# Two convolution banks emptied by ScalarE alone: offsets in the base's upper channels, the odd half through SBUF

## The chip, the cores and the metric

One core of a Trainium2 chip (trn2) runs the whole program. The metric is the device time of one execution in microseconds. Five engines work side by side, each in the order of its own program: PE (TensorE, matrix products; its weight loads are shown apart as PEld), DVE (VectorE), ACT (ScalarE), POOL (GpSimd) and SP (SyncE, which here only issues DMAs). They wait for each other through semaphores.

## What is computed

Two layers over 32 images of 96 x 56 x 56. The first is an inverted bottleneck (1x1 to 576 channels, 3x3 depthwise, squeeze and excite, 1x1 back to 96). The second attends in channels and space by the magnitudes of a Fourier transform, and then mixes a plain and a deformable 3x3 convolution. The change touches only this part of the second layer:

```
aux = concatenate([y, coord, freq_e], 1)                  # 96 + 5 channels
offset = conv3x3(aux, off_w, off_b)                       # 18 channels
gate = sigmoid(conv1x1(relu(conv3x3(aux, dg1_w, dg1_b)), dg2_w, dg2_b))   # 50 hidden
y_base = conv3x3(y, base_w, base_b)                       # 96 channels
y_def = deformable 3x3 convolution of y at the offsets    # 96 channels
z = (1 - gate) * y_base + gate * y_def
out = relu(batchnorm(z) + x)
```

All data is float32.

## The kernel before

**Images and bands.** An image is cut into 7 bands of 8 rows (448 pixels), so there are 224 bands. A band passes three stages: the *joint and base convolutions* that make its hidden gate values, its offsets and its base (two bands ahead of their use); the *sampling*, in two halves, in which small matrix products with bilinear weights (L718) make the values at the offset positions; and the *deformable product* (L737) with the combination (L776 to L779). Beside the bands of image b run the attention of image b+1 (L387, L408 and what follows; its projection is L325, L331, L335, L463) and the depthwise convolution of image b+2: L166 on PE expands, L170 on ACT applies SiLU, L257 and L259 on DVE add the nine taps (long instructions over 128 x 1568), and L219 on ACT finishes a unit after its last tap.

**Order.** The program is written as generators that are stepped side by side: `offsets` for a band is stepped once for every tile of the sampling, and after each step `pump` advances the other streams by their share. The order on PE, DVE, ACT and POOL is then set by the framework's list scheduler from dependencies and priorities; on SP it is the order of the text. On each engine it is fixed when the program is built: an instruction that waits holds up all behind it.

**PSUM.** All products but three kinds go to the pool `mm` of six banks (`bank`), which are handed out in turn. A matmul into a bank waits until the last reader of its former contents is done.

**The joint convolution** (`joint_conv`, L617 to L635). Nine taps (L602, `conv3`) over 104 channels (96 of y, 5 auxiliary ones, 3 planes that add each pixel's place and the offsets' bias) fill one bank of 128 rows: rows 0 to 49 the hidden values, rows 64 to 81 the 18 offsets (`OFF0` is 64), rows 96 to 127 the base's last 32 channels (`QC` is 32; `BC` is 64). ACT takes the hidden values out (L622) and, in a later step, the 32 base channels with their bias (L625, into `yb`). DVE takes out the offsets in two strided copies of 18 x 224 (L648, into `at`). ACT's L625 comes after DVE's copies, since both read one bank.

**The base convolution** of the first 64 channels (L630) lets even taps add up in rows 0 to 63 of a second bank and odd taps in rows 64 to 127. ACT takes out the even half with the bias (L633, into `yb[:64]`); in the next step DVE adds the odd half straight from the bank (L635). So the last reader of the first bank is ACT's L625 and that of the second bank is DVE's L635.

**The way of the offsets.** After L648 POOL issues a DMA of the offsets to DRAM (L652, `od`); SP loads them back broadcast (L664, `ht`), ACT turns them into weights per axis (L667, L668), ACT's queue stores these (L671, `hd`), SP loads them as column and row weights (L682, L683: `wc`, `wr`), and DVE multiplies the two (L689). That product is an input of the sampling L718. L659 on DVE keeps the largest offset (`top`), which decides at the end of all bands whether a general path must run.

**Others that the prediction names.** L700 (POOL) and L704 (PE) cut y into blocks and transpose them; L706 (ACT) empties those two banks. L722 (ACT) empties the banks of L718, L729 (ACT) packs part of the values, and both feed L737. L394 (ACT) is a PSUM copy of the transform, L482 and L483 (DVE) are two small SBUF copies of the attention, L274 (`sa`) and L518 (`cx`) late DVE steps of the attention, after which L528 on PE goes on.

Of the kernel before, what the change touches and what calls it, by code (L numbers as in the profile page):

```python
# [7 lines left out]
FP = mybir.dt.float32  # L8
I32 = mybir.dt.int32
AF = mybir.ActivationFunctionType  # L10
ALU = mybir.AluOpType
# [5 lines left out]
C, H, W = 96, 56, 56  # L17
# [9 lines left out]
CA = C + 5  # L27
CJ = CA + 3
NOFF, NTAP = 18, 9
# [5 lines left out]
NBD = H // RB  # L35
BW = NBW
TS = 4
NTX = W // TS
NTH = NTX // 2
TP = TS * TS  # L40
GROUPS = ((0, 3),), ((3, 5), (5, 7))
REACH = PD
SB = TS + 2 * REACH
NS = SB * SB
KP = NTAP * TP
BC = 64
QC = 32
KA = 7
DMID = CA // 2
OFF0 = 64  # L50
MAUX = OFF0 + NOFF
MID = C // 4
PT = 2 * W
# [61 lines left out]
def bank(p):  # L115
    return p["mm"].tile([128, 512], FP, name="mm")
# [479 lines left out]
def conv3(nc, out, weights, yp, channels, j):  # L596

    view = out.rearrange("p (h w) -> p h w", h=RB)
    for k in range(NTAP):
        dy, dx = divmod(k, 3)  # L600
        r0 = j * RB + dy + PD - 1
        nc.tensor.matmul(view, weights[:, k], yp[:channels, r0 : r0 + RB, dx + PD - 1 : dx + PD - 1 + W],  # L602
                         start=(k == 0), stop=(k == NTAP - 1))


def aux_conv(nc, p, yp, j):

    w = p["w"]
    pa = bank(p)
    conv3(nc, pa[:MAUX, :BW], w["aux"], yp, CA, j)  # L610
    hid = p["hid"].tile([DMID, BW], FP, name="hid")
    nc.scalar.activation(hid, pa[:DMID, :BW], AF.Relu, bias=w["dg1b"])
    return hid, pa[OFF0 : OFF0 + NOFF, :BW]


def joint_conv(nc, p, yp, j, hid):


    w = p["w"]
    pa = bank(p)  # L620
    conv3(nc, pa[:, :BW], w["joint"], yp, CJ, j)
    nc.scalar.activation(hid, pa[:DMID, :BW], AF.Relu, bias=w["dg1b"][:DMID])  # L622
    yb = p["yb"].tile([C, BW], FP, name="yb")
    yield yb, pa[OFF0 : OFF0 + NOFF, :BW]
    nc.scalar.activation(yb[BC:], pa[OFF0 + QC :, :BW], AF.Identity, bias=w["cv"]("base_b")[BC:])  # L625
    pb = bank(p)
    for k in range(NTAP):
        dy, dx = divmod(k, 3)
        r0 = j * RB + dy + PD - 1
        nc.tensor.matmul(pb[k % 2 * BC : (k % 2 + 1) * BC, :BW].rearrange("p (h w) -> p h w", h=RB), w["base"][:, k],  # L630
                         yp[:C, r0 : r0 + RB, dx + PD - 1 : dx + PD - 1 + W], start=(k < 2), stop=(k > NTAP - 3))
    yield
    nc.scalar.activation(yb[:BC], pb[:BC, :BW], AF.Identity, bias=w["cv"]("base_b")[:BC])  # L633
    yield
    nc.vector.tensor_tensor(yb[:BC], yb[:BC], pb[BC:, :BW], ALU.add)  # L635


def offsets(nc, p, yp, j, top, hid, ybs, hds):

    w = p["w"]
    joint = joint_conv(nc, p, yp, j, hid)
    yb, pa = next(joint)
    ybs.append(yb)
    at = p["off"].tile([NOFF, NTX, 2, TP], FP, name="at")
    for s in range(2):
        nc.vector.tensor_copy(at[:, :, s].rearrange("o t (r c) -> o t r c", r=TS),  # L648
                              pa[:, s * BW // 2 : (s + 1) * BW // 2].rearrange("o (r t c) -> o t r c", r=TS, t=NTX))
    yield  # L650
    od = p["dp"].tile([NTX, 2, NOFF, TP], FP, name="od")
    nc.gpsimd.dma_start(od.rearrange("t s o p -> o (t s) p"), at.rearrange("o t s p -> o (t s) p"))  # L652
    yield
    next(joint)
    yield
    next(joint)
    yield
    next(joint, None)
    nc.vector.tensor_reduce(top, at.rearrange("o t s p -> o (t s p)"), AX.X, ALU.max, apply_absolute_value=True)  # L659
    for _ in range(4):  # L660
        yield
    ht = p["ht"].tile([SB * NTX, 4, KP], FP, name="ht")
    src = od.rearrange("t s o p -> t (s o p)").unsqueeze(0).to_broadcast([SB, NTX, 4 * KP])
    nc.sync.dma_start(ht.rearrange("q n k -> q (n k)"), src)  # L664
    for _ in range(6):
        yield
    p["tc"].keep_in_program_order(nc.scalar.activation(ht, ht, AF.Abs, bias=w["blk"]))  # L667
    nc.scalar.activation(ht, ht, AF.Relu, bias=w["one"], scale=-1.0)  # L668
    yield
    hd = p["dp"].tile([4, SB, NTX, KP], FP, name="hd")  # L670
    nc.scalar.dma_start(hd.rearrange("x i t n -> (i t) x n"), ht)  # L671
    hds.append(hd)
# [100 lines left out]
def combine(nc, p, j, pd, yb, gate, st):  # L773

    z = p["q2"].tile([C, BW], FP, name="z")
    nc.vector.scalar_tensor_tensor(z, pd[:C, :BW], p["w"]["cv"]("def_b"), yb, ALU.add, ALU.subtract)  # L776
    nc.vector.scalar_tensor_tensor(z, gate, 1.0, z, ALU.add, ALU.mult)
    nc.vector.scalar_tensor_tensor(z, z, 0.5, yb, ALU.mult, ALU.add)
    nc.vector.bn_stats(st[:, j], z)  # L779
    return z  # L780
# [132 lines left out]
def padded(nc, p, a, images):  # L913

    cp = p["cp"]
    yps = [cp.tile([CJ, HY, WY], FP, name=f"yp{i}") for i in range(images)]
    for t in yps:
        nc.gpsimd.memset(t, 0.0)
        nc.sync.dma_start(t[C : C + 4, PD : PD + H, PD : PD + W], a["coord"])
        nc.sync.dma_start(t[CA:, PD : PD + H, PD : PD + W], a["place"])  # L920
    p["s4"] = [cp.tile([H, 3, WP], FP, name=f"s4_{i}") for i in range(2)]
    for t in p["s4"]:
        nc.gpsimd.memset(t, 0.0)
    return yps


def pools(tc, ctx, p, space, sizes):
    for name, bufs in sizes:
        kw = {"space": space} if space else {}
        p[name] = ctx.enter_context(tc.tile_pool(name=f"l1{name}", bufs=bufs, **kw))  # L930


def layers(tc, a, dp, x1d, zd, stats, far):
# [6 lines left out]
    nc = tc.nc  # L940
    B = x1d.shape[0]
    with ExitStack() as ctx:
        p = {"tc": tc, "dp": ctx.enter_context(tc.tile_pool(name="l1d", bufs=3, space=DRAM))}
# [1 line left out]
        hidden_constants(tc, ctx, a, p)  # L945
        constants(tc, ctx, a, p)
        yp, = padded(nc, p, a, 1)
        top = p["cp"].tile([NOFF, NBD + 1], FP, name="top")
        nc.gpsimd.memset(top, 0.0)
        pools(tc, ctx, p, None, (("xt", 2), ("acch", 2), ("pl", 2), ("w3s", 1), ("hq", 9), ("o", 2), ("x2", 3),  # L950
                                 ("ca", 2), ("s1p", 1), ("xc", 2), ("sp", 1), ("sq", 1), ("q1", 3), ("q2", 2), ("hid", 2), ("yb", 4),
                                 ("off", 1), ("st", 2), ("ht", 1), ("wc", READY + AHEAD + 1), ("wr", AHEAD + 1), ("yt", 2), ("ybl", 1),
# [86 lines left out]
        def store(b, j, z):  # L1039
            nc.gpsimd.dma_start(zd[b][:, j * BW : (j + 1) * BW], z)  # L1040

        def join(n, pd, gate, st):
            b, j = bands[n]
            z = combine(nc, p, j, pd, ybs[n], gate, st)
            later.append((slot + 7, lambda: store(b, j, z)))
            if j == NBD - 1:
                nc.vector.bn_aggr(stats[:, b], st)
# [19 lines left out]
        bands = [(b, j) for b in range(B) for j in range(NBD)]  # L1067
        hids, gates, ybs, hds, ready = [], [], [], [], []

        def find(n):  # L1070
            if n % 2 == 0:
                hids.append(p["hid"].tile([2 * NS, BW], FP, name="hid"))
            hid = hids[n // 2][n % 2 * NS : n % 2 * NS + DMID]
            return offsets(nc, p, yp, bands[n][1], top[:, n % NBD : n % NBD + 1], hid, ybs, hds)

        for n in range(2):
            for _ in beside(find(n)):
# [21 lines left out]
        for n, (b, j) in enumerate(bands):  # L1099
            if j == 0:  # L1100
                st = p["st"].tile([C, NBD, 6], FP, name="st")
# [7 lines left out]
            for h in range(2):  # L1109
                v = p["vp"].tile([128, NTAP, NTH, 2, TP], FP, name="v")  # L1110
                prepare(2 * n + h + READY + AHEAD)
                s = ready.pop(0)
# [17 lines left out]
                if h == 0:  # L1130
                    if n % 2 == 0:
                        gates.extend(gates_of(nc, p, hids[n // 2]))
                    gate = gates.pop(0)
# [11 lines left out]
            end()  # L1145
        flush()

        every = p["cp"].tile([NOFF, 1], FP, name="every")
        nc.gpsimd.partition_all_reduce(every, top[:, NBD:], NOFF, bass_isa.ReduceOp.max)
        nc.vector.tensor_scalar(far, every, (SB - 1) / 2, None, ALU.is_gt)  # L1150


def locate(nc, p, yp, j):
# [200 lines left out]
def _arrays(inp):  # L1354
# [10 lines left out]
    A = {"x": np.ascontiguousarray(inp["x"])}  # L1365
# [12 lines left out]
    l1 = {k[len("L1_conv_"):]: np.asarray(v) for k, v in inp.items() if k.startswith("L1_conv_")}  # L1378
    A["baseW"] = np.ascontiguousarray(l1["base_w"].reshape(C, C, 9).transpose(1, 2, 0))
    aux = np.zeros((CA, 9, MAUX), f)  # L1380
    aux[:, :, :DMID] = l1["dg1_w"].reshape(DMID, CA, 9).transpose(1, 2, 0)
    aux[:, :, OFF0:] = l1["off_w"].reshape(9, 2, CA, 9).transpose(2, 3, 1, 0).reshape(CA, 9, NOFF)
    A["auxW"] = aux
    joint = np.zeros((CJ, 9, 128), f)
    joint[:CA, :, :MAUX] = aux
    for xy in range(2):
        joint[CA + xy, 4, OFF0 + xy * NTAP : OFF0 + (xy + 1) * NTAP] = 1.0
    joint[CA + 2, 4, OFF0 : OFF0 + NOFF] = l1["off_b"].reshape(9, 2).T.reshape(NOFF)
    joint[:C, :, OFF0 + QC :] = A["baseW"][:, :, BC:]
    A["jointW"], A["base0W"] = joint, np.ascontiguousarray(A["baseW"][:, :, :BC])  # L1390
    A["defW"] = np.ascontiguousarray(l1["def_w"].reshape(C, C, 9).transpose(1, 2, 0))
    cp1 = np.concatenate([l1["cp1_w"][:, :, 0, 0]] * 2)
# [24 lines left out]
    t = 2 * np.pi * np.outer(np.arange(H), np.arange(V)) / H  # L1417
    A["FU"] = np.kron(np.eye(2), np.concatenate([np.cos(t), -np.sin(t)], 1) / np.sqrt(H * W)).astype(f)
    t = 2 * np.pi * np.outer(np.arange(W), np.arange(W)) / W
# [29 lines left out]
    at = (np.arange(W) + 0.5) * V / W - 0.5  # L1449
# [20 lines left out]
    t = (np.arange(W) % TS + REACH - mid).astype(f)  # L1470
# [22 lines left out]
```

## Time and profile before

| | us |
|---|---|
| median of 3 runs | 9719.62 |
| lowest, highest | 9716.68, 9745.26 |
| the profiled execution: time, span | 9756.57, 9754.8 |
| mean granted TensorE clock in it | 0.927 |

The instruction groups of the profile that the change touches, and the longest on DVE (a row has line, engine, operation, operands, count, busy us and mean ns):

| line | engine, operation | count | busy us | mean ns |
|---|---|---|---|---|
| L259 | DVE, taps of the depthwise convolution | 2250 | 4329.5 | 1924 |
| L602 | PE, joint convolution | 4032 | 1641.0 | 559 |
| L630 | PE, base convolution | 4032 | 913.7 | 550 |
| L622 | ACT, hidden values out of the bank, 50x448 | 224 | 140.6 | 628 |
| L625 | ACT, 32 base channels out of the bank, 32x448 | 224 | 140.3 | 627 |
| L633 | ACT, even half out of the bank, 64x448 | 224 | 140.2 | 626 |
| L635 | DVE, odd half added from the bank, 64x448 | 224 | 138.2 | 617 |
| L648 | DVE, offsets out of the bank, 18x224 | 448 | 156.6 | 380 |

Times of the trace are counted from the start of the profiled execution's span. A matrix product in float32 shows as two records on PE. Waits are named by the instruction that waits and the one whose end let it go.

### The profile page before, as it was taken

The numbers are of one execution on the slowest core, as the hardware profiler recorded it, in microseconds if no ns is written. First come the engines' busy times: TensorE is split into PE (matmuls) and PEld (weight loads), VectorE is DVE, ScalarE is ACT, GpSimd is POOL, SyncE is SP. The second block draws the span as 40 slices with busy tenths as digits, with TensorE's granted clock in tenths as the row PEclk, the third lists the DMA queues.
The fourth block names the chain that finished last, engine by engine and source line by source line (L and its number), as shares of the span: only waits on it lengthen the run. The fifth ranks groups of instructions, "written<-read, shape, count | busy, mean of one in ns | idle before, by whom it ended". The sixth has DMA issues, their size and how long they took to land. (4 is left out here: it accounts for less than half of the span.)

```text
span 9754.8 us, 122161 instructions
## 1 busy us (share of the span) xinstructions
PE 8671.3 (89%) x43766; PEld 5043.0 (52%) x43766; DVE 7253.6 (74%) x6948; ACT 5336.3 (55%) x10262; POOL 2537.1 (26%) x2639
## 2 busy tenths in 40 slices
PE   6889999999999999999999999999999999999970
PEld 3455555555555555555555555555555555555540
DVE  7688777777777777877777787778778777877323
ACT  2355555555555555555555555555555555565453
POOL 0133222322322222222232322223222322322210
PEclk9889999999999999999999999999999999999985
DMA  3345555554555555555555555555555555555449
GB/s 93 110 134 143 157 148 157 151 151 134 145 154 151 156 146 143 138 151 151 156 154 147 142 142 151 153 153 152 148 141 147 153 156 150 153 148 137 129 151 416
DMA packets 1083658, 1485.55 MB, mean 152 GB/s; under 512 B 604742, under 2 KB 854294, under 8 KB 1070758
## 3 DMA queue, kind: packets, MB, share of 16 engines
q1 hardware_dynamic: 873083, 985.26, 37.3%
q10 hardware_dynamic: 153675, 329.79, 9.2%
q0 software_dynamic: 56288, 162.60, 6.7%
q8 instruction: 352, 5.77, 0.3%
q14 instruction: 260, 2.13, 0.1%
HBM read 1064.28 MB, written 412.65 MB: 151 GB/s over the span
## 5 line engine op out<-in xcount | busy, mean ns | idle before, releaser
L259 DVE SCALAR_TENSOR_TENSOR acch<-hp,w,acch 128x1512 f32<-128x1512 f32 (+1 forms) x2250 | 4329.5, 1924 | 35.3
L602 PE MATMUL mm<-yp,c_jointW 104*128 104x448 f32 x4032 | 1641.0, 559 | 3.7 <-DMA yp<-fqd 3.4
L737 PE MATMUL pd<-v,c_def 128*96 128x224 f32 (+1 forms) x6272 | 1451.7, 382 | 142.0 <-ACT v L729 114.5
L700 POOL COPY ybl<-yp 96x448 f32<-96x448 f32 x896 | 1014.3, 1159 | 2042.8 <-PE mm L704 2042.1
L718 PE MATMUL mm<-wc,yt 64*96 64x144 f32 x12544 | 1162.5, 306 | 233.1 <-DVE yb L635 157.4
L737 PEld LDWEIGHTS pd<-v,c_def 128*96 128x96 f32 (+1 forms) x6272 | 1069.2, 176 | 463.1 <-ACT v L729 153.6
L166 PE MATMUL mm<-xt,w 96*128 96x392 f32 (+3 forms) x2688 | 1119.4, 553 | 111.0 <-ACT yt L706 55.6
L602 PEld LDWEIGHTS mm<-yp,c_jointW 104*128 104x128 f32 x4032 | 781.0, 195 | 789.7 <-issue 745.8
L718 PEld LDWEIGHTS mm<-wc,yt 64*96 64x96 f32 x12544 | 881.5, 166 | 568.8 <-issue 192.9
L219 ACT ACTIVATE acch<-acch,sh,inv 128x1568 f32<-128x1568 f32 x288 | 487.5, 1693 | 1237.1 <-DVE acch L259 1209.7
L722 ACT COPY v<-mm 96x288 f32<-96x288 f32 (+1 forms) x2688 | 1004.7, 441 | 203.9 <-PE mm L718 161.0
L689 DVE TENSOR_TENSOR wc<-wc,wr 128x1008 f32<-128x1008 f32 x448 | 545.6, 1218 | 745.0 <-DMA wr<-hd 672.5
L170 ACT ACTIVATE hp<-mm,sh,inv 128x392 f32<-128x392 f32 (+2 forms) x1216 | 810.3, 671 | 388.2 <-PE mm L166 338.3
L630 PE MATMUL mm<-yp,c_base0W 96*64 96x448 f32 x4032 | 913.7, 550 | 0.0
L325 PE MATMUL mm<-hq,w3s 128*96 128x392 f32 x2048 | 766.8, 519 | 90.8 <-DMA hq<-h2d 41.2
L729 ACT COPY v<-v 32x448 f32<-32x448 f32 x1344 | 755.1, 562 | 29.8
L652 POOL DMA_DIRECT2D od<-at x224 | 185.9, 830 | 2223.4 <-DVE at L648 1506.9
L408 PE MATMUL mm<-s,c_GV 112*112 112x464 f32 x1536 | 664.2, 574 | 0.0
L166 PEld LDWEIGHTS mm<-xt,w 96*128 96x128 f32 (+1 forms) x2688 | 390.2, 187 | 493.5 <-issue 273.6
L706 ACT COPY yt<-mm 128x384 f32<-128x384 f32 (+1 forms) x896 | 352.1, 440 | 490.6 <-PE mm L704 488.6
L257 DVE TENSOR_SCALAR acch<-hp,w 128x1568 f32<-128x1568 f32 x270 | 296.5, 1098 | 418.4 <-ACT hp L170 418.4
L463 POOL TENSOR_TENSOR o<-o,xc 96x392 f32<-96x392 f32 x256 | 399.3, 1560 | 722.7 <-ACT o L335 721.0
(193 smaller groups left out, 8937.5 us busy)
## 6 DMA issues: line engine op xcount, KB each, us to landing
h2d<-acch ACTq DMA_DIRECT2D x288, 784.0 KB
hq<-h2d SPq DMA_DIRECT2D x1152, 196.0 KB
wc<-hd SPq DMA_DIRECT2D x896, 252.0 KB
wr<-hd SPq DMA_DIRECT2D x896, 252.0 KB
x<-x1d SPq DMA_DIRECT2D x768, 98.0 KB
ht<-od SPq DMA_DIRECT2D x224, 252.0 KB
hd<-ht ACTq DMA_DIRECT2D x224, 252.0 KB
xt<-in_x SPq DMA_DIRECT2D x64, 609.0 KB
```

The lines of the kernel that those rows point to most:

```text
L166: nc.tensor.matmul(pt[p0 : p0 + w1.shape[1], : rows * W], w1, xts[hf][:, r0 * W : (r0 + rows) * W], start=True, stop=True)
L170: nc.scalar.activation(h1[lo:hi, row0 : row0 + rows, 1 : 1 + W], pt[lo:hi, : rows * W].rearrange("p (h w) -> p h w", h=rows), AF.Silu, bia ...
L259: nc.vector.scalar_tensor_tensor(acc[:, lo:hi], win, wk, acc[:, lo:hi], ALU.mult, ALU.add)
L325: nc.tensor.matmul(pts[half][:C, :EW], w3s[:, ch], hq, start=(i == 0), stop=False)
L408: nc.tensor.matmul(pt[: 2 * W, :n].rearrange("p (q u) -> p q u", q=NPB), w["GV"][:, g], m, start=(k == 0), stop=(k == 1))
L602: nc.tensor.matmul(view, weights[:, k], yp[:channels, r0 : r0 + RB, dx + PD - 1 : dx + PD - 1 + W], start=(k == 0), stop=(k == NTAP - 1))
L630: nc.tensor.matmul(pb[k % 2 * BC : (k % 2 + 1) * BC, :BW].rearrange("p (h w) -> p h w", h=RB), w["base"][:, k], yp[:C, r0 : r0 + RB, dx + ...
L700: nc.gpsimd.tensor_copy(yb[:, :, s], blocks)
L718: nc.tensor.matmul(pt[k][:C, (t - lo) * KP : (t - lo + 1) * KP], yt[ps, t], s[ps, t * KP : (t + 1) * KP], start=True, stop=True)
L722: nc.scalar.copy(v[:C, :, lo:hi, k].rearrange("c k t p -> c t k p"), pt[k][:C, : (hi - lo) * KP].rearrange("c (t k p) -> c t k p", t=hi - ...
L729: nc.scalar.copy(v[C:, 1 + 2 * i : 3 + 2 * i], v[i * QC : (i + 1) * QC, KA:])
L737: nc.tensor.matmul(out.rearrange("c q (t x) -> c t q x", x=TS), p["w"]["def"][ks, k], v[ks, k].rearrange("c t s (r x) -> c t (s r) x", r=T ...
```

## The change

The joint bank is laid out anew: hidden values in rows 0 to 49 as before, the base's last 32 channels in rows 64 to 95, and the offsets in rows 96 to 113 (`JOFF` is 96). One ACT instruction now takes both out of the bank into a `yb` of 114 rows, right after the hidden values and before the first step ends; its bias (`jbias`) is 0 for the offsets. In the next step DVE's two copies take the offsets from `yb` instead of the bank. The DMA of the offsets and the base convolution's matmuls are issued in one step, the third.

ACT also takes out the base bank's odd half, as a second copy into 64 rows of a tile `off`, whose rows 96 to 113 hold the copied offsets; DVE's add then reads SBUF alone. `top` and the last reduction over it grow to 114 rows, of which 18 are used, and the weights are laid out to match.

```diff
+JOFF = C
-def joint_conv(nc, p, yp, j, hid):
+def joint_conv(nc, p, yp, j, hid, odd):
     nc.scalar.activation(hid, pa[:DMID, :BW], AF.Relu, bias=w["dg1b"][:DMID])
-    yb = p["yb"].tile([C, BW], FP, name="yb")
-    yield yb, pa[OFF0 : OFF0 + NOFF, :BW]
-    nc.scalar.activation(yb[BC:], pa[OFF0 + QC :, :BW], AF.Identity, bias=w["cv"]("base_b")[BC:])
+    yb = p["yb"].tile([JOFF + NOFF, BW], FP, name="yb")
+    nc.scalar.activation(yb[BC:], pa[BC : JOFF + NOFF, :BW], AF.Identity, bias=w["jbias"][BC:])
+    yield yb
     pb = bank(p)
...
     yield
-    nc.scalar.activation(yb[:BC], pb[:BC, :BW], AF.Identity, bias=w["cv"]("base_b")[:BC])
+    nc.scalar.activation(yb[:BC], pb[:BC, :BW], AF.Identity, bias=w["jbias"][:BC])
+    nc.scalar.copy(odd, pb[BC:, :BW])
     yield
-    nc.vector.tensor_tensor(yb[:BC], yb[:BC], pb[BC:, :BW], ALU.add)
+    nc.vector.tensor_tensor(yb[:BC], yb[:BC], odd, ALU.add)
 def offsets(nc, p, yp, j, top, hid, ybs, hds):
-    joint = joint_conv(nc, p, yp, j, hid)
-    yb, pa = next(joint)
+    off = p["off"].tile([JOFF + NOFF, BW], FP, name="off")
+    at = off[JOFF:].rearrange("o (t s p) -> o t s p", t=NTX, s=2)
+    joint = joint_conv(nc, p, yp, j, hid, off[:BC])
+    yb = next(joint)
     ybs.append(yb)
-    at = p["off"].tile([NOFF, NTX, 2, TP], FP, name="at")
+    yield
     for s in range(2):
         nc.vector.tensor_copy(at[:, :, s].rearrange("o t (r c) -> o t r c", r=TS),
-                              pa[:, s * BW // 2 : (s + 1) * BW // 2].rearrange("o (r t c) -> o t r c", r=TS, t=NTX))
+                              yb[JOFF:, s * BW // 2 : (s + 1) * BW // 2].rearrange("o (r t c) -> o t r c", r=TS, t=NTX))
     yield
...
     nc.gpsimd.dma_start(od.rearrange("t s o p -> o (t s) p"), at.rearrange("o t s p -> o (t s) p"))
-    yield
     next(joint)
     yield
 def layers(tc, a, dp, x1d, zd, stats, far):
-        top = p["cp"].tile([NOFF, NBD + 1], FP, name="top")
+        top = p["cp"].tile([JOFF + NOFF, NBD + 1], FP, name="top")
         nc.gpsimd.memset(top, 0.0)
+        p["w"]["jbias"] = p["cp"].tile([JOFF + NOFF, 1], FP, name="jbias")
+        nc.gpsimd.memset(p["w"]["jbias"], 0.0)
+        nc.vector.tensor_copy(p["w"]["jbias"][:C], p["w"]["cv"]("base_b"))
...
-            z = combine(nc, p, j, pd, ybs[n], gate, st)
+            z = combine(nc, p, j, pd, ybs[n][:C], gate, st)
...
-        every = p["cp"].tile([NOFF, 1], FP, name="every")
-        nc.gpsimd.partition_all_reduce(every, top[:, NBD:], NOFF, bass_isa.ReduceOp.max)
+        every = p["cp"].tile([JOFF + NOFF, 1], FP, name="every")
+        nc.gpsimd.partition_all_reduce(every, top[:, NBD:], JOFF + NOFF, bass_isa.ReduceOp.max)
 def _arrays(inp):
-    joint[:CA, :, :MAUX] = aux
+    joint[:CA, :, :DMID] = aux[:, :, :DMID]
+    joint[:CA, :, JOFF : JOFF + NOFF] = aux[:, :, OFF0:]
...
-    joint[:C, :, OFF0 + QC :] = A["baseW"][:, :, BC:]
+    joint[:C, :, BC:C] = A["baseW"][:, :, BC:]
```

## The prediction

> **What bounds the kernel.** First the page's busy row and clock row, then the table of waits, then the timeline of one place and the granted clock there.
>
> ```profile
> PE 8671.3 (89%) x43766; PEld 5043.0 (52%) x43766; DVE 7253.6 (74%) x6948; ACT 5336.3 (55%) x10262; POOL 2537.1 (26%) x2639
> PEclk9889999999999999999999999999999999999985
> ```
> PE is the fullest engine, but not alone: its clock row stays at nine tenths, so some of its busy time is run slowly. Which engine ends its waits (us in total, times, longest; the last row is from SyncE's own list):
> ```profile
> PE mm L718 <- DVE yb L635: 157.4, 47, 5.8
> PE pd L737 <- ACT v L729: 114.5, 71, 4.3
> ...
> ACT acch L219 <- DVE acch L259: 1209.7, 200, 11.3
> ...
> ACT yb L625 <- DVE at L648: 306.8, 94, 7.2
> ...
> SPq L664 <- DMA od<-at: 720.4, 73, 14.9
> ```
> The first row is what the change aims at: PE waits 157.4 us for a bank of the base convolution, because DVE's add L635, its last reader, stands behind long taps (L259, 1.9 us each). The third row is the one to fear: ScalarE, in order, waits 1209.7 us at L219 for DVE's last tap, and every bank it has yet to empty waits too. The 157.4 us fall almost wholly in two of an image's seven bands: the third (counted from 0: band 2), some 5 us in most images, and band 5, under 1 us. Band 2 of one image (us from the start, duration, engine):
> ```profile
> 4517.19 8.93 DVE L259 SCALAR_TENSOR_TENSOR acch<-hp,w,acch 128x1568 f32<-128x1568 f32 x4
> 4517.44 0.62 ACT L633 ACTIVATE yb<-mm,c_cvec 64x448 f32<-64x448 f32 x1
> ...
> 4520.33 0.78 ACT L706 COPY yt<-mm 128x384 f32<-128x384 f32 x2 [1.66 <-PE mm L704]
> ...
> 4526.04 0.61 DVE L635 TENSOR_TENSOR yb<-yb,mm 64x448 f32<-64x448 f32 x1
> 4526.58 1.84 DVE L259 SCALAR_TENSOR_TENSOR acch<-hp,w,acch 128x1568 f32<-128x1568 f32 x1
> 4526.71 1.27 PE L718 MATMUL mm<-wc,yt 64*96 64x144 f32 x6 [5.27 <-DVE yb L635]
> 4527.91 1.67 PE L166 MATMUL mm<-xt,w 96*128 96x392 f32 x2
> ...
> 4528.45 1.70 ACT L219 ACTIVATE acch<-acch,sh,inv 128x1568 f32<-128x1568 f32 x1 [7.34 <-DVE acch L259]
> ```
> DVE works without a gap from 4517 to 4530; PE waits 5.27 us for the add, and 1.8 us later ScalarE gets out of its own wait for the same DVE. The stall costs twice; the windows table (stretch, its length, busy PE, PEld, DVE, ACT, POOL, then the clock) shows PE at half clock after it, though always busy from 4528:
> ```profile
> 4512.00:4517.00 5.00, 5.00 (x24) 1.77 (x21) 4.95 (x6) 1.32 (x3) 0.83 (x1) 1.00 0.00 0
> 4526.00:4528.00 2.00, 1.29 (x7) 0.96 (x7) 2.00 (x3) 0.00 (x0) 0.54 (x1) 0.50 0.70 141
> 4534.00:4536.00 2.00, 2.00 (x5) 1.13 (x6) 0.12 (x1) 2.00 (x5) 0.00 (x0) 0.50 0.52 158
> 4538.00:4540.00 2.00, 2.00 (x17) 1.71 (x16) 1.21 (x1) 0.34 (x1) 0.00 (x0) 1.00 0.58 233
> ```
> The clock records put half clock here from 4524.1 to 4537.8 (13.65 us); after all 29 such band-2 stalls of the steady part they add up to 440 us.
>
> **The change, part by part.** I compared the order of instructions on each engine in the two built programs. SP's is the same; POOL's and PE's move in a few places; on ScalarE and DVE a few instructions change places, and these decide.
>
> *The odd half through SBUF (ODD).* 224 copies of 64x448 from PSUM are added to ScalarE. Nearest row: L394, 112x464, median 545 ns; 16 elements fewer make about 0.53 us, 224 x 0.53 = 119 us. In the trace, after L633 ScalarE idles at least 0.55 us before it reaches anything PE waited for, in all but 3 of 224 bands (mostly waiting for the transposes of L704, as in the 1.66 above). So that idle time hides it: cost 0; with the cover gone up to 119 us.
>
> *The add L635 and the bank.* The add now reads two SBUF tensors; PE no longer waits for it. By itself that takes 157.4 us of waits away (153.5 if each ends 0.55 us after L633). But what is late next in band 2? PE's sequence there is L718 (eight matmuls), then L166, whose bank is the one that L706 empties (six banks rotate). In the program before, L706 stands behind L219 in every second image (kind A) and ahead of it in the others (kind B, the timeline above). In the changed program L706 stands behind L219 **in every image**. The trace of before shows what that means: in all 15 A images L166 starts 0.41 us after ScalarE's accumulator read that ends L219, and in the B images mostly 2.33 us before it. So:
> - B, 14 images: L718 runs 5 us sooner, which is of no use, and L166 starts at +0.41 instead of -2.33: 2.74 us later. PE then rests from about 4522 to 4530.7, and works at half clock from there. Phases after A stalls are mostly 17.1 us, after B mostly 13.7; half of the 3.4 us would be 1.7, and if recovery is counted from when PE resumes, only 0.6: I take 1.0.
> - A, 15 images: the add moves behind the last tap, so L219 starts 0.61 us sooner (the add's duration), and L166 with it.
>
> *A rule that speaks against the add.* The Trainium skill, "SBUF — State Buffer", section "Who interferes with whom", says that a DVE instruction with two SBUF inputs contends with a GpSimd instruction that reads SBUF, and that the later one is blocked. Rows: the add with a PSUM input is flat, 607 to 624 ns; L689, with two SBUF inputs, goes from 1183 to 1995 ns. By the row of before the add stays 0.62; by the rule it may grow by up to 0.8, and in B a POOL copy (L700) does run beside it, ahead of the tap that L219 waits for. I take 0.3 there, 0 to 0.8 as ends; elsewhere DVE's idle 2500 us cover it.
>
> *Offsets out of yb.* L648's two copies read SBUF instead of PSUM. L648: median 378 ns for 224 elements; L482, a strided SBUF copy of 192, median 251, L483 with 48, 200: about 260 to 270 for ours, 0.22 us saved per band (ends: 0.4 saved, or 0.4 lost to the same blocking, L482's longest being 626). On the path in band 2: -0.22 in A and B. The ScalarE activation they now wait for (50 instead of 32 partitions, same 0.63 us) runs straight after hid L622, ahead of L722: behind it two L722 copies come 0.63 later, but they no longer have L625 and its 306.8 us of waiting after them. That wait overlaps PE's idle time by 0.05 us only; POOL, whose next work (o L463) stands behind the od DMA and so behind the same copies, gives ScalarE's earlier results no earlier use: gain 0.
>
> *od later.* POOL's order stays, so the DMA follows the copies. Where SP waits for od (bands 3 and 4, the 720.4 us), SP's hq, wc and wr loads queue behind it, and DVE's L689 behind those. Band 3: in every second image one DVE z (0.68 us) now precedes the copies; 0.68 - 0.22 = 0.46 us, x 15 = 7 us. Band 4: the copies stand one tap (1.9 us) and a few small steps (0.3) later, but DVE idled 1.39 us on average there for hid: it fills that idle time. od is about 0.8 later, while the chain to cx L518 is 1.4 shorter; PE's wait for L518 (23.5 us, 29 times) bounds the gain at 0.8 an image, and later in the band another tap is put ahead of sa L274, up to 1.9 lost less the 1.2 idle before it. I take -0.4 x 30 = -12 us, between -24 and +20.
>
> *Start-up* (one 96x1 copy, one memset) and the end (114 instead of 18 partitions in one reduction): under 1 us.
>
> **Sum.** B: 14 x (2.74 + 1.0 + 0.3 - 0.22) = 14 x 3.82 = +53. A: 15 x (-0.61 - 0.22) = -12. Bands 3 and 4: +7 - 12 = -5. Together +36 us. Against the profiled execution (span 9754.8, time 9756.6) that is 9792; the median of the runs is 9719.6, 37 us below that execution, and +36 makes **9755**, +0.37%. What a measurement of this kernel can tell from no change is about 0.3%, 29 us.
>
> *The clock, by rule and by row.* The skill's "TensorE: Matmul & The Clock Gate", section "Part 1: The HAM clock gate", has the clock back after about 3.4 us of sustained work. The trace shows 11 us (4526.7 to 4537.8). If the stalls really vanished, the row would give back half of 11 us x 29 = 160 us beside the 153, the rule 49.
>
> **Rivals.**
> 1. *The stalls go as meant* (not slower): PE's first wait, 5 us at L718, is no longer there, and if L219's tap came early enough that L166 weren't held, 9720 - 153 - 160 = about 9405 by the row, 9520 by the rule. For: the wait row itself. Against: L219 still waits for a busy DVE, and L706 stands behind it. It decides only if DVE comes some 7 us sooner. Chance 0.07.
> 2. *DVE's filled idle time wins* (not slower): in bands 4 and 5 the 1.39 and 1.2 us are filled and the 2.4 us that PE waits at L718 behind L219 in band 5 (one of the L722 waits) shrink too: 2.5 x 30 = 75 saved, less the 41 of B and A: 9685. Against: z L776 in band 5 waits for PE anyway. It decides from 1.4 us an image. Chance 0.19, of which 0.14 faster by more than 0.3%.
> 3. *The extra ScalarE copies are not hidden*: in the A-like order PE's L737 and L718 wait for L729 and L722 (114.5 and 58.8 us now), each 0.53 later or more: +119 on top of 36 gives 9875; half of it, 9815. Against: the cover counted above. Chance 0.16.
> 4. The forecast case: 0.58, own range 9720 to 9790; 0.37 of it slower by over 0.3%, 0.21 within.
>
> That the change doesn't free the bank is no rival: in the built program no matmul's order or bank depends on the add any more.
>
> Chances: slower 0.37 + 0.16 = 0.53; within 0.3%: 0.21 + 0.05 = 0.26; faster 0.14 + 0.07 = 0.21. The range leaves out rival 1 and the far end of rival 3: 9650 to 9840.
>
> **What would show it.** The row "PE L718 <- DVE yb" gone, and in its place about 30 waits of 7 to 9 us at L166 for L706 or L219 in band 2; L166 0.4 us after L219's accumulator read in all images; half-clock phases of 17 us after them; ScalarE's wait at L625 gone and its wait at L219 longer; 224 copies of about 0.53 us; L648 at 270 ns, and an add that varies with POOL. I am wrong if the band-2 wait of PE is gone or short, if L219 starts microseconds sooner, or if waits for L722 and L729 grow by 100 us.

## The result and the profile after

| | before | after |
|---|---|---|
| median of 4 runs, us | 9718.15 | 9809.34 |
| lowest, highest, us | 9714.75, 9745.26 | 9789.23, 9830.65 |
| span of the profiled execution, us | 9754.8 | 9807.5 |
| mean granted clock in it | 0.927 | 0.924 |

The changed kernel is slower: ratio 1.0089, 95% interval 1.0069 to 1.0109. The medians are 91 us apart; the two profiled executions are only 53 apart, since that of before lies 38 us above its own median. Line numbers after L48 grew by 1 to 4 in the part shown here: the taps are now L260, the finish L220, the expansion L167, the odd copy L635, the add L637, the offset copies L652, `wc` L692, GpSimd's `ybl` copies L703, the transposes L707, the `yt` copies L709, the sampling L721.

The page's busy row and clock row after the change:

```profile
PE 8627.7 (88%) x43766; PEld 5005.4 (51%) x43766; DVE 7249.6 (74%) x6949; ACT 5459.9 (56%) x10486; POOL 2796.3 (29%) x2640
PEclk9889999999999999999999999999999999999985
```
PE, DVE and the clock row hardly moved. ScalarE has 124 us more, 119 of it the odd copies. But GpSimd, which got no work in the bands, is busy 259 us longer. The table of waits (us in total, times, longest), first of PE, then one row each of ScalarE's and DVE's own tables:

```profile
PE mm L167 <- ACT yt L709: 267.4, 53, 9.2
PE pd L740 <- ACT v L732: 99.3, 77, 5.4
PE mm L388 <- POOL x L368: 64.5, 38, 5.7
PE mm L707 <- POOL ybl L703: 47.8, 21, 3.8
...
ACT acch L220 <- DVE acch L260: 1209.2, 186, 10.4
...
DVE yb L637 <- ACT off L635: 204.5, 99, 6.0
```
The row that the change aimed at, PE waiting 157.4 us for DVE's add, is gone. In its place stands the first row (55.6 us before). Two rows that name GpSimd grew from 39.5 and 2.6 us: the prediction has nothing of them. ScalarE's own wait in the finish did not change (1209.7 before). The groups of the new and moved instructions (busy us, mean ns, then idle time before them):

```profile
L703 POOL COPY ybl<-yp 96x448 f32<-96x448 f32 x896 | 1318.2, 1497 | 1977.0 <-PE mm L707 1976.9
...
L637 DVE TENSOR_TENSOR yb<-yb,off 64x448 f32<-64x448 f32 x224 | 148.1, 661 | 204.8 <-ACT off L635 204.5
...
L635 ACT COPY off<-mm 64x448 f32<-64x448 f32 x224 | 118.6, 529 | 5.1
L652 DVE COPY off<-yb 18x224 f32<-18x224 f32 x448 | 118.6, 298 | 221.7 <-ACT yb L625 217.3
```
The odd copy takes 529 ns, as estimated. The same 896 `ybl` copies, on the same shapes, now take 1497 ns on average, against 1159. Counted in the traces, 7 of them took over 5 us before and 91 do after, 55 of these in band 4 (29 in the image kind A of the next paragraph, 26 in B).

**Where the time went.** I measured, in both traces, the time from the start of one band's base convolution to that of the next, and averaged it over 15 pairs of images (B is the image kind with L706 ahead of L219 before, A the other):

| stretch that starts at band | B, us per image | A, us per image |
|---|---|---|
| 0 | +2.26 | -0.12 |
| 1 | +0.45 | -0.36 |
| 2 | -0.55 | -1.54 |
| 3 | +0.32 | +2.18 |
| 4 | -1.85 | **+5.14** |
| 5 | -2.37 | -1.17 |
| 6 | -0.18 | +0.26 |

Together +2.4 us a pair, 15 x 2.4 = 37 us of the 53; the start and the last images hold the rest. Band 2, where the prediction put its +53 and -12, became shorter in both kinds, and bands 1 to 3 together are close to zero (+0.22 and +0.28). The loss stands above all in two other places: band 0 of B (15 x 2.26 = 34 us) and band 4 of A (15 x 5.14 = 77 us), and -4.2 us in bands 4 and 5 of B (63 us) pays back part of it. Band 3 of A takes back what band 2 gave: PE's waits at the expansion there grew from 12.0 to 24.0 us over the 15 images, and its busy time at half clock from 3.1 to 5.7 us an image. No run here isolates why.

**Band 4 of A.** In 14 of 15 images the stretch is 37.9 to 38.2 us long (before: 32.4 to 33.4). The timeline of one, first before, then after (start, duration, engine, what it waited for):

```profile
4904.29 2.97 POOL L700 COPY ybl<-yp 96x448 f32<-96x448 f32 x2 [6.72 <-PE mm L704]
4904.40 0.68 DVE L776 SCALAR_TENSOR_TENSOR z<-pd,c_cvec,yb 96x448 f32<-96x448 f32 x1
4905.00 1.84 DVE L259 SCALAR_TENSOR_TENSOR acch<-hp,w,acch 128x1568 f32<-128x1568 f32 x1
4906.76 0.97 DVE L777 SCALAR_TENSOR_TENSOR z<-gate,z 96x448 f32<-96x448 f32 x1
```

```profile
4926.33 0.67 DVE L779 SCALAR_TENSOR_TENSOR z<-pd,c_cvec,yb 96x448 f32<-96x448 f32 x1
4926.41 0.78 ACT L709 COPY yt<-mm 128x384 f32<-128x384 f32 x2 [0.64 <-PE mm L707]
4926.76 10.70 POOL L703 COPY ybl<-yp 96x448 f32<-96x448 f32 x2 [6.81 <-PE mm L707]
4926.93 1.84 DVE L260 SCALAR_TENSOR_TENSOR acch<-hp,w,acch 128x1568 f32<-128x1568 f32 x1
4928.69 0.61 DVE L780 SCALAR_TENSOR_TENSOR z<-gate,z 96x448 f32<-96x448 f32 x1
4929.22 1.84 DVE L260 SCALAR_TENSOR_TENSOR acch<-hp,w,acch 128x1568 f32<-128x1568 f32 x1
...
4935.20 3.84 DVE L260 SCALAR_TENSOR_TENSOR acch<-hp,w,acch 128x1568 f32<-128x1568 f32 x2
...
4937.51 0.63 PE L707 MATMUL mm<-c_ident,ybl 96*128 96x96 f32 x5 [1.66 <-POOL ybl L703]
```
Two GpSimd copies, 2.97 us before, take 10.70 after, while DVE goes from instruction to instruction without a gap from 4926 to 4937. The second ends at 4937.46, 0.4 us behind the boundary between the last two taps (the row with x2). PE then starts the transposes late, and the clock halves. Windows of that stretch, one before and three after (stretch, length, busy PE, PEld, DVE, ACT, POOL, clock, then the DMA's share and GB/s):

```profile
4914.00:4918.00 4.00, 3.93 (x41) 2.64 (x40) 3.96 (x4) 2.83 (x10) 2.87 (x2) 1.00 0.36 121
...
4936.00:4940.00 4.00, 2.49 (x19) 1.75 (x19) 3.01 (x2) 1.53 (x5) 3.05 (x4) 0.85 0.61 160
4940.00:4944.00 4.00, 4.00 (x31) 2.72 (x27) 2.51 (x4) 1.97 (x6) 0.00 (x0) 0.50 0.16 47
4944.00:4948.00 4.00, 4.00 (x7) 2.14 (x7) 3.08 (x4) 3.16 (x7) 0.00 (x0) 0.50 0.00 0
```
PE works on for some 10 us at half clock (9.56 us an image on average; none before), which costs about half of that, by estimate: 4.8 of the 5.1 us. The long copies in band 4 of B cost nothing that can be seen: PE has no wait for them there, and the stretch is shorter than before. What costs is PE's wait behind a copy, and not the copy's length.

**Band 0 of B.** DVE's lines around the scaling of the projection's weights (`w3s`), before and after:

```profile
4443.24 0.17 DVE L292 TENSOR_SCALAR s<-s 128x5 f32<-128x5 f32 x1 [0.27 <-ACT s L291]
4443.45 0.66 DVE L294 TENSOR_TENSOR w3s<-w,s 128x480 f32<-128x480 f32 x1
...
4450.61 1.21 DVE L689 TENSOR_TENSOR wc<-wc,wr 128x1008 f32<-128x1008 f32 x1 [6.50 <-DMA wr<-hd]
```

```profile
4465.26 0.17 DVE L293 TENSOR_SCALAR s<-s 128x5 f32<-128x5 f32 x1 [0.27 <-ACT s L292]
4471.55 1.21 DVE L692 TENSOR_TENSOR wc<-wc,wr 128x1008 f32<-128x1008 f32 x1 [6.11 <-DMA wr<-hd]
4472.67 0.65 DVE L295 TENSOR_TENSOR w3s<-w,s 128x480 f32<-128x480 f32 x1
...
4473.43 2.84 PE L326 MATMUL mm<-hq,w3s 128*96 128x392 f32 x8 [1.81 <-ACT v L725]
```
In the changed program DVE stands 6.11 us at `wc` for a load, with `w3s` ready and queued behind it, and PE's projection L326 waits for `w3s` (the table names ScalarE, whose work had been done; PE starts with `w3s`). Before, the two stood the other way round in every B image and this way in every A image; after the change, this way in all 29 images of the steady part.

### The profile page after: what moved, and what is told of

Same layout as the page of the kernel before. It is cut to its first block, busy times and chain, and to the rows that moved or that the text cites. A ratio compares the mean times of both kernels' runs of the same rounds, so it can differ in the third digit from the quotient of the medians.

```text
span 9807.5 us, 122820 instructions
## 1 busy us (share of the span) xinstructions
PE 8627.7 (88%) x43766; PEld 5005.4 (51%) x43766; DVE 7249.6 (74%) x6949; ACT 5459.9 (56%) x10486; POOL 2796.3 (29%) x2640
## 5 line engine op out<-in xcount | busy, mean ns | idle before, releaser
L260 DVE SCALAR_TENSOR_TENSOR acch<-hp,w,acch 128x1512 f32<-128x1512 f32 (+1 forms) x2250 | 4341.0, 1929 | 38.5
L703 POOL COPY ybl<-yp 96x448 f32<-96x448 f32 x896 | 1318.2, 1497 | 1977.0 <-PE mm L707 1976.9
L740 PE MATMUL pd<-v,c_def 128*96 128x224 f32 (+1 forms) x6272 | 1418.7, 375 | 127.1 <-ACT v L732 99.3
L167 PE MATMUL mm<-xt,w 96*128 96x392 f32 (+3 forms) x2688 | 1134.8, 560 | 309.3 <-ACT yt L709 267.4
L740 PEld LDWEIGHTS pd<-v,c_def 128*96 128x96 f32 (+1 forms) x6272 | 1046.3, 173 | 432.7 <-ACT v L732 139.9
L721 PE MATMUL mm<-wc,yt 64*96 64x144 f32 x12544 | 1119.6, 307 | 65.3 <-ACT v L725 32.2
L220 ACT ACTIVATE acch<-acch,sh,inv 128x1568 f32<-128x1568 f32 x288 | 487.2, 1692 | 1229.7 <-DVE acch L260 1209.2
L692 DVE TENSOR_TENSOR wc<-wc,wr 128x1008 f32<-128x1008 f32 x448 | 543.3, 1213 | 726.5 <-DMA wr<-hd 603.8
L721 PEld LDWEIGHTS mm<-wc,yt 64*96 64x96 f32 x12544 | 864.8, 167 | 391.6 <-issue 186.0
L326 PE MATMUL mm<-hq,w3s 128*96 128x392 f32 x2048 | 774.5, 524 | 101.9 <-DMA hq<-h2d 40.2
L656 POOL DMA_DIRECT2D od<-off x224 | 185.9, 830 | 2195.2 <-DVE off L652 1899.4
L167 PEld LDWEIGHTS mm<-xt,w 96*128 96x128 f32 (+1 forms) x2688 | 396.6, 190 | 696.6 <-issue 299.0
L709 ACT COPY yt<-mm 128x384 f32<-128x384 f32 (+1 forms) x896 | 351.0, 440 | 499.3 <-PE mm L707 495.3
L464 POOL TENSOR_TENSOR o<-o,xc 96x392 f32<-96x392 f32 x256 | 364.4, 1423 | 729.1 <-ACT o L336 727.0
```

What stands on the lines that cost most here:

```text
L167: nc.tensor.matmul(pt[p0 : p0 + w1.shape[1], : rows * W], w1, xts[hf][:, r0 * W : (r0 + rows) * W], start=True, stop=True)
L260: nc.vector.scalar_tensor_tensor(acc[:, lo:hi], win, wk, acc[:, lo:hi], ALU.mult, ALU.add)
L326: nc.tensor.matmul(pts[half][:C, :EW], w3s[:, ch], hq, start=(i == 0), stop=False)
L703: nc.gpsimd.tensor_copy(yb[:, :, s], blocks)
L721: nc.tensor.matmul(pt[k][:C, (t - lo) * KP : (t - lo + 1) * KP], yt[ps, t], s[ps, t * KP : (t + 1) * KP], start=True, stop=True)
L740: nc.tensor.matmul(out.rearrange("c q (t x) -> c t q x", x=TS), p["w"]["def"][ks, k], v[ks, k].rearrange("c t s (r x) -> c t (s r) x", r=T ...
```

## The experiments

Each ran in five rounds beside the kernel before. Ratios are to the kernel before, with 95% intervals; the runs of one group shared its executions.

**The parts alone.** `e1_joint` keeps only the joint bank's part, `e2_odd` only the odd half's.

```diff
 # e1_joint, against the changed kernel
-    nc.scalar.copy(odd, pb[BC:, :BW])
-    nc.vector.tensor_tensor(yb[:BC], yb[:BC], odd, ALU.add)
+    nc.vector.tensor_tensor(yb[:BC], yb[:BC], pb[BC:, :BW], ALU.add)
 # e2_odd, against the kernel before
+    nc.scalar.copy(odd, pb[BC:, :BW])
-    nc.vector.tensor_tensor(yb[:BC], yb[:BC], pb[BC:, :BW], ALU.add)
+    nc.vector.tensor_tensor(yb[:BC], yb[:BC], odd, ALU.add)
```

> The joint bank's part alone: offsets leave with the base's last channels, the odd half is still added from PSUM, no extra ScalarE copies. In the built program L219 stands ahead of the yt copies in band 2 of every image, as in the changed kernel. Theory A (the place of L219 makes the loss): slower than before by 30 to 80 us, with PE waiting at the base's sampling for DVE's add and then at the expansion for L219. Theory B (GpSimd is shut out by DVE's denser order, which this part brings): near the changed kernel, 9790 to 9810, with ybl copies of over 5 us in the fourth and fifth band. Theory C (the 224 extra copies or the SBUF add make the loss): within 15 us of before.

> The odd half's part alone: ScalarE copies it to SBUF, the add reads SBUF, offsets leave as before. L219 stays behind the yt copies in band 2 of every second image. Theory A: in these 14 images PE no longer waits 5 us for the add and nothing is late in its place, 14 x (5 + half of some 7 us of half clock) = about 110 us faster, 9600 to 9640. Theory B: the SBUF add alone adds little, so a gain too, but less, as DVE's idle gaps are filled: 9640 to 9720. Theory C: slower than before by 40 us or more.

Measured: `e1_joint` 9744.94 us, 1.0008 (0.9998 to 1.0017); `e2_odd` 9762.65 us, 1.0026 (1.0016 to 1.0037). The parts don't add up to 1.0089. `e1_joint` has the finish ahead of the `yt` copies in every image, and loses nothing: against theory A, and as theory C said of this run. `e2_odd` has the extra copies and the SBUF add, and loses about a third of the whole, less than C's 40 us and the wrong way for A and B; so C is not the main cause. No stretch of its trace stands out, and where that third goes is open. Neither has an `ybl` copy of over 5 us in band 4, nor `wc` ahead of `w3s` in B: the loss of these two places needs both parts, because only together do they bring that order and that timing.

**The finish behind the `yt` copies.** `e3_finish_late` on the changed kernel, `e4_finish_late_before` on that of before. `issue_after` sets only the order on the engine, and no wait.

```diff
-        nc.scalar.copy(yt[:, lo:hi]..., pt[:, : (hi - lo) * C])
+        p.setdefault("yc", []).append(nc.scalar.copy(yt[:, lo:hi]..., pt[:, : (hi - lo) * C]))
...
+        with tc.issue_after(p["yc"][-3].ins) if u == 2 and "yc" in p else ExitStack():
             nc.scalar.activation(flat, flat, AF.Silu, ...)
```

> The changed kernel with one edit: the finish of unit 2 (L219 of before) is put behind the two yt copies that it overtook in band 2, in every image; nothing else moves in that band. Theory A: PE's wait of 8 to 9 us at the expansion goes in all images, 30 x (5 to 6 us + half of 9 to 14 us of half clock) = 280 to 380 us faster than the changed kernel, 9430 to 9530. If PE is then held behind the sampling copies that stand behind the finish, only half: about 9650. Theory B: the waits go too, but the loss in bands 0, 3 and 4 stays, so this kernel stays 40 us or more above the unchanged kernel with the same edit.

> The kernel before with the same edit, so that the finish of unit 2 stands behind the yt copies in every image and not in every second. PE still waits for DVE's add. Theory A: the images of the one kind become like the other: a few us each, 9680 to 9720, and 150 us or more above the changed kernel with this edit. Theory B: at most equal to the changed kernel with this edit, since the loss of the change lies elsewhere.

Measured: `e3_finish_late` 9804.54 us, 1.0088 (1.0066 to 1.0110), the changed kernel's own ratio; `e4_finish_late_before` 9733.40 us, 0.9996 (0.9985 to 1.0008). Theory A falls: the order that the prediction called decisive was undone, and the time stayed. (In `e4_finish_late_before`, A images gain 2.82 us in band 2 and lose 2.48 in band 3, as in the changed kernel.) PE's waits in `e3_finish_late` show why:

```profile
PE mm L722 <- ACT v L726: 138.7, 33, 7.7
...
PE mm L764 <- ACT v L726: 82.0, 14, 7.2
...
PE mm L167 <- ACT yt L710: 40.4, 25, 2.0
```
The 267 us at the expansion are down to 40, but 138.7 and 82.0 us stand at the next products, whose banks are emptied by copies behind the same finish. The hold was moved, not removed.

**The two places.** `e5_w3s_first` puts `wc` behind `w3s`; `e6_ybl_scalar` has ScalarE make the two copies that GpSimd is shut out of, in A and B (in the code they belong to the sampling of band 3, which begins in the stretch of band 4); `e7_both` has both; `e9_w3s_first_before` has the first edit on the kernel before.

```diff
 # e5, e7, e9
-    nc.vector.tensor_tensor(w3s, ...)
+    p["w3m"] = nc.vector.tensor_tensor(w3s, ...)
...
-                        ready.extend(weights(nc, *ws) for ws in loads[:1])
+                        w3m = p.pop("w3m", None)
+                        with tc.issue_after(w3m.ins) if w3m else ExitStack():
+                            ready.extend(weights(nc, *ws) for ws in loads[:1])
 # e6, e7
-        nc.gpsimd.tensor_copy(yb[:, :, s], blocks)
+        if (j, h) == (3, 0):
+            nc.scalar.copy(yb[:, :, s], blocks)
+        else:
+            nc.gpsimd.tensor_copy(yb[:, :, s], blocks)
```

> The changed kernel with one edit: DVE's product wc (1.2 us and its wait for loads) is put behind the scaling of the projection's weights (w3s) in band 0 of every image; in the program before it stood behind it in every second image, in the changed kernel in none. Theory D (the loss sits in two places of the built order): band 0 gets back its 2.3 us in 14 images, 32 us less than the changed kernel, ratio to before 1.005 to 1.006; bands 3 and 4 stay as they are. Rival E (the loss is the sum of many small ones, the 224 copies among them): no more than 10 us, 1.008 or 1.009.

> The changed kernel with one edit: in band 4 of each image the two ybl copies that GpSimd needs 5.3 and 5.4 us for are made by ScalarE; the order on DVE stays. Theory D: these copies take about 0.6 us, the 5.1 us of band 11 (band 4 of every second image) and its 9.6 us of half clock go, about 75 us less than the changed kernel, ratio to before 1.001 to 1.003. Rival E, or if the late z and taps of DVE hold the band whatever GpSimd does: within 15 us of the changed kernel.

> The changed kernel with both edits of the two runs before. Theory D: the gains add, about 105 us less than the changed kernel, ratio to before 0.997 to 1.000. Rival E: 1.007 or more.

> The kernel before with wc put behind w3s in every image, as in the changed kernel's run. There it already stood so in band 0 of one kind of image, so only the other kind (band 7 of a pair) can gain. The run on the changed kernel got 4.2 us there against the kernel before and 1.9 in the other kind. Theory D: 15 x 4.2 = 63 us less than before, ratio 0.993 to 0.995; then about 30 us of what that run regained was taken back from the change, and about 60 was a gain open to both kernels. Rival: within 20 us of before, and all that the run regained belonged to the change.

| run | median, us | ratio (interval) | band 0 of B | band 0 of A | band 4 of A |
|---|---|---|---|---|---|
| changed kernel | 9809.34 | 1.0089 (1.0069 to 1.0109) | +2.26 | -0.12 | +5.14 |
| `e5_w3s_first` | 9726.44 | 0.9999 (0.9978 to 1.0020) | +0.35 | -4.23 | +5.04 |
| `e6_ybl_scalar` | 9740.07 | 1.0016 (1.0006 to 1.0027) | +1.50 | +0.32 | +0.47 |
| `e7_both` | 9678.02 | 0.9948 (0.9928 to 0.9968) | +0.34 | -4.24 | +0.37 |
| `e9_w3s_first_before` | 9640.02 | 0.9921 (0.9908 to 0.9934) | 0.00 | -4.53 | +0.59 |

(The last three columns are us per image against the trace of before, as above.) Each edit takes away most or all of the loss of its own place (in `e6_ybl_scalar` band 0 of B shrank somewhat too) and leaves most of the other, and the two nearly add: 0.90% and 0.73% alone, 1.41% together. Rival E falls. In `e6_ybl_scalar` the copies take 0.55 us each, in the same DVE order:

```profile
4888.11 0.55 ACT L704 COPY ybl<-yp 96x448 f32<-96x448 f32 x1
4888.81 0.55 ACT L704 COPY ybl<-yp 96x448 f32<-96x448 f32 x1
```
`e5_w3s_first` gained 83 us where 32 were expected, and `e7_both` came out below its expected range, because the edit also helps the A images, where `wc` stood first already before. `e9_w3s_first_before` prices that on the kernel before: 73 us less (9713.50 in its group), somewhat more than the 63 expected. So of what e5 regained, about 15 x (2.26 - 0.35) = 29 us was the change's loss; the rest was open to both kernels.

With both places mended, `e7_both` is still 0.27% (26 us) above `e9_w3s_first_before`, the intervals just touching. So the change gains nothing yet, and a remainder is left. Its largest piece in the trace is a third place where GpSimd is shut out: band 6 of A, 2.19 us longer than before. Of the row of `e7_both` below, 59 us fall there, in 11 images (before: none there):

```profile
PE mm L710 <- POOL ybl L706: 67.7, 14, 9.2
```

**The copy kept, its result unread.** The output is the same as before.

```diff
-    nc.vector.tensor_tensor(yb[:BC], yb[:BC], odd, ALU.add)
+    nc.vector.tensor_tensor(yb[:BC], yb[:BC], pb[BC:, :BW], ALU.add)
```

> The changed kernel, with the odd half's copy to SBUF still made by ScalarE, but the add reads the bank again, so DVE no longer waits for that copy (0.55 us more than for the even half) and reads one SBUF tensor instead of two. The built order has the wc product behind w3s again in every second image. Theory D, with the later add as what shuts GpSimd out (DVE reaches z 0.5 us later, and no longer has to wait there for PE): no ybl copies of 5 us in band 4, ratio to before 1.000 to 1.003. If the copies' place in DVE's order and not its lateness shuts GpSimd out: 1.005 to 1.007. Rival E (the copies on ScalarE cost): 1.007 or more.

Measured: 9714.64 us, 0.9995 (0.9984 to 1.0006). `e1_joint` is this kernel without the 224 copies, at 1.0008: so the copies on ScalarE cost nothing that can be measured. And with neither of the two bad places the change is level with before. But the reason given in the expectation fell. The add still waited for the copy and started 5.57 us into the stretch, as in the changed kernel, and GpSimd was not shut out:

```profile
4876.90 0.68 DVE L779 SCALAR_TENSOR_TENSOR z<-pd,c_cvec,yb 96x448 f32<-96x448 f32 x1
4877.21 5.21 POOL L703 COPY ybl<-yp 96x448 f32<-96x448 f32 x2 [6.75 <-PE mm L707]
4877.50 1.83 DVE L260 SCALAR_TENSOR_TENSOR acch<-hp,w,acch 128x1568 f32<-128x1568 f32 x1
4879.26 0.97 DVE L780 SCALAR_TENSOR_TENSOR z<-gate,z 96x448 f32<-96x448 f32 x1
```
DVE has the same order here as in the changed kernel. GpSimd comes 0.31 us behind the start of `z` instead of 0.43, and gets in at L780, which takes 0.97 us instead of 0.61. What lets it in there and not 0.12 us later is not settled.

**The finish out of ScalarE's way.** With both edits, the finish of unit 2 goes behind the first half's `pack` (which now returns its last copy) (`e10_finish_behind_pack`), or to the end of band 2 (`e11_finish_end_of_band`); `e12_finish_end_before` has the `w3s` edit and the latter on the kernel before.

```diff
-                pack(nc, v)
+                p.setdefault("pk", []).append(pack(nc, v))
...
 # e11 and e12; e10 has [-2]
+        with tc.issue_after(p["pk"][-1].ins) if u == 2 and len(p.get("pk", [])) > 1 else ExitStack():
             nc.scalar.activation(flat, flat, AF.Silu, ...)
```

> The changed kernel with the two edits (w3s first, two ybl copies on ScalarE), and the finish of unit 2 put behind the first half's pack in band 2, so behind all that PE waits for at that place and not behind the yt copies alone. Theory F (PE's stall in band 2 is ScalarE's wait for DVE in the finish, whatever stands behind it): PE's 8 to 9 us of idle time and its 9 to 14 us of half clock in band 2 go in 30 images, 200 to 350 us less than with the two edits alone, 9330 to 9480. A finish of band 3 moves ahead of the sampling copies there and may give back a third. Rival G (DVE sets the pace here, PE only waits elsewhere): within 40 us of the two edits alone, 9640 to 9720.

> The same, but the finish of unit 2 goes to the end of band 2, and band 3 stays as it is. Theory F: as the run before or better, 9330 to 9450, unless the unit that takes over the finished accumulator waits for it. Rival G: within 40 us of the two edits alone, 9640 to 9720.

> The kernel before with the same two edits to the order: w3s first, and the finish of unit 2 at the end of band 2 (its GpSimd copies need no edit, they are not shut out there). Theory H (the bank that ScalarE alone empties is worth something only once the finish is out of ScalarE's way): PE still waits 4 to 5 us for DVE's add in band 2 of every image, so little is gained over w3s first alone, 9600 to 9650, some 100 us or more above the changed kernel with the edits (9503). Rival I (the edits do it all, the change is worth nothing): 9480 to 9530.

Measured: `e10_finish_behind_pack` 9634.25 us, 0.9909 (0.9893 to 0.9925); `e11_finish_end_of_band` 9503.04 us, 0.9780 (0.9765 to 0.9795); `e12_finish_end_before` 9570.52 us, 0.9831 (0.9812 to 0.9850). In e10 a finish of band 3 did move ahead of the sampling copies, and the gain over `e7_both` is 0.4%, 38 us: alone it would fit theory G. In e11 PE's idle time in band 2 falls from 8.6 (B) and 9.5 us (A) in `e7_both` to 4.9 and 6.6, the profiled span from 9678.3 to 9496.9, and PE's first waits are of another kind:

```profile
PE pd L745 <- DVE z L784: 123.9, 34, 5.9
PE pd L745 <- ACT v L736: 108.7, 73, 4.8
```
That is 1.7% below `e7_both`, some 160 us. Theory F's 200 us and more did not come whole; PE now waits 123.9 us for DVE's `z`, which holds the one bank of the deformable product. Theory G, which allowed 40, falls. And e12 lies between its two theories: the finish's new place gains 0.9% on the kernel before and 1.7% on the changed one. On the kernel before PE still waits for the add:

```profile
PE mm L719 <- DVE yb L636: 161.2, 47, 5.9
```
So the change is worth some 0.5% (e11 against e12) once the finish is no longer what comes next. Two thirds of what separates the two traces lie in band 2 (1.8 us an image in B, 1.4 in A), where that wait stands; this fits the freed bank as the reason, but no run takes the bank alone. `e11_finish_end_of_band` is the fastest of all kernels run, 2.2% below the kernel before.

## Why the prediction was right, and where it was not

The direction was right and the time lies in the range, but not by its own sum, and in good part by luck: +36 was forecast; +53 between the profiled executions and +91 between the medians came, and from other places.

- **The wait that goes and the one that takes its place: right.** PE's wait for the add is gone; the expansion starts 0.41 or 0.42 us behind the finish's accumulator read in all 29 images of the steady part, with waits of 5.4 to 9.2 us, mostly 7 to 9. Band 2 of one B image after:

```profile
4546.05 1.22 PE L721 MATMUL mm<-wc,yt 64*96 64x144 f32 x16
4549.01 0.97 DVE L637 TENSOR_TENSOR yb<-yb,off 64x448 f32<-64x448 f32 x1
4551.78 1.69 ACT L220 ACTIVATE acch<-acch,sh,inv 128x1568 f32<-128x1568 f32 x1 [7.87 <-DVE acch L260]
4553.38 0.19 ACT L220 ACTIVATION_READ_ACCUMULATOR acch<-acch,sh,inv 128x1 f32 x1
4553.98 1.67 PE L167 MATMUL mm<-xt,w 96*128 96x392 f32 x2 [6.70 <-ACT yt L709]
```
- **B, +53 us: failed.** PE did start later (idle time in band 2 of B 8.37 us against 5.34, as 2.74 + 0.3 said), but the stretch became 0.55 us shorter, and bands 1 to 3 of B came to +0.22 us an image. Two terms of "B: 14 x (2.74 + 1.0 + 0.3 - 0.22)" were wrong. The clock term has the wrong sign: the half-clock phases shrank from mostly 13.7 to 10.2 us in B and from 17.1 to 13.7 in A, where 17 was expected in all. And "L718 runs 5 us sooner, which is of no use" was wrong too: before, part of its products ran at half clock after the stall (clock 0.50 from 4526 to 4528 in the prediction's windows); after, as in the lines above, all 16 records run ahead of it, and half clock begins only at 4549.7. Together, PE's busy time at half clock in that stretch fell from 10.8 to 5.4 us an image; half of the difference, 2.7 us, is an estimate of what that gave back, where 1.0 was to be lost. That `e3_finish_late` undoes the step and keeps the ratio agrees.
- **A, -12 us:** -0.83 was forecast for band 2 and -1.54 came, but with it +2.18 in band 3, where at most 0.46 was forecast; +0.28 us an image over bands 1 to 3.
- **The odd copies at no cost: right** (529 ns; `e8_copy_unread` against `e1_joint`).
- **The rule on two SBUF inputs: the page was right, the victim was the wrong one.** The add grew from 617 to 661 ns on average: to about 0.97 us in 30 of 224 bands, in all of which a GpSimd copy ran beside it (8 of 16 images in band 2 of B, 15 of 16 in its band 3), so there by about the 0.3 us taken. But the Trainium skill's "SBUF — State Buffer", section "Who interferes with whom", says it of both engines. I priced what GpSimd does to one short DVE instruction, and not what a denser DVE does to GpSimd: 77 us in band 4 of A.
- **Bands 3 and 4, -5 us: failed as a size on one side and in sign on the other.** In B, bands 4 and 5 came out 4.2 us shorter, with the waits that rival 2 named going (in the 15 B images together 24.8 us behind the finish in band 5, and half of 17.2 for `cx` in band 4); in A, with DVE's gaps filled, GpSimd was shut out, and band 4 grew by 5.14 us where a small gain stood in the sum.
- **A sign that did not come:** ScalarE's wait in the finish was to be longer, and stayed (1209.7 and 1209.2 us).
- **Band 0: missing.** The prediction says that the few exchanged instructions on DVE decide, and follows those of bands 2 to 5. The exchange of `wc` and `w3s` in band 0 was in the built order to be read, and would have been priced from before's own A images, which had it already.
- **L648:** 272 ns in the median (298 on average, the longest 1120) against 260 to 270: right but for a few long ones.

## What to carry to other kernels

A change to a few instructions under a list scheduler is priced by its whole new order: walk through every exchanged pair on every engine, ask which of the two waits for a load, and look for a place of the old kernel that has that order already. An order of "ready but queued behind a wait" on an in-order engine (`w3s` behind `wc`, every copy behind the finish) is worth more here than the bank that the change freed; only after those were put right did the change pay (e11 against e12). And when DVE's gaps are filled, look at what GpSimd was doing in them.

## What the hardware showed that was not expected

- **GpSimd can be shut out over many DVE instructions.** A copy that takes 0.55 us alone took up to 7.6 us, in single cases in the kernel before too. The Trainium skill's "SBUF — State Buffer", section "Summary: rules for kernel authors", says that the second of two such instructions is blocked until the first is finished; here it waited through up to seven instructions of DVE. For the `ybl` copies of over 1.5 us in the changed kernel I looked at each boundary between two DVE instructions that they waited through: 499 were passed without getting in, and at each of them DVE's next instruction had begun 69 to 94 ns before the record of the last one ended. Wherever DVE had a gap, of 31 ns or more as between two taps of one accumulator, GpSimd got in. At some 150 boundaries without a gap it got in too; why is open.
- **The half clock comes in steps, and lasts.** The phases in band 2 of these kernels are 3.4, 6.8, 10.2, 13.7, 17.1 or 20.5 us long, multiples of 3.41 (the Trainium skill's "TensorE: Matmul & The Clock Gate", "Part 1: The HAM clock gate", gives its window as 3413 ns). But they go on over several windows in which PE is busy throughout: PE's wait of 1.66 us in band 4 of A, amid small products, was followed by 10.2 us of it (4938.8 to 4949.0), in all of which PE was busy. `e6_ybl_scalar`, without that wait, has 1.8 us of half clock in that stretch instead of 9.56.
